# One-hot products in the order of the equalities, and the routing table's end half a step sooner, in a mixture-of-experts kernel on one core

## The chip, the cores and the metric

The kernel runs on one core of a Trainium2 chip. The metric is the time of one execution in microseconds (us) on the device. The engines of the core are named as in the profile: PE (TensorE, matmuls), PEld (its weight loads), DVE (VectorE), ACT (ScalarE), POOL (GpSimd) and SP (SyncE, which issues DMAs). L564 is line 564 of the kernel.

## The reference

`x` has 64 x 64 tokens of 256 numbers; each goes to 2 of 8 experts, and the result is added to `x`:

```python
xn = rms_w * (x * rsqrt(mean(x * x) + 1e-6))
gate_w = softmax(xn @ wg_W + wg_b + (cond @ gg_W + gg_b))     # 8 experts
topk_w, topk_i = top_k(gate_w, 2)
cw = sum(one_hot(topk_i) * topk_w)                            # weight of each expert
h1 = relu(x @ W1[e] + b1[e])                                  # 256 -> 512
h2 = relu(h1 @ W2[e] + b2[e])                                 # 512 -> 512
out = x + sum_e(cw[e] * (h2 @ W3[e] + b3[e]))                 # 512 -> 256
```

All inputs and the output are float32.

## The kernel before

**Tiles and units.** The kernel computes an expert only for the tokens that chose it. Tokens are sorted by expert into tiles of 128, and tiles into units of one expert. Units 0 to 7 (`E = 8`) are single tiles, one for each expert, made of the tokens of a first part (a quarter of all), which is routed first. The rest is routed while units 0 to 6 are computed, and gives units 8 and up, of 1 to 4 tiles each. A unit's rows are fetched from HBM by POOL's indirect DMAs (`gather`, `gather_unit`, L771), turned (for unit 8 by eight PE transposes, L836; for later units by a round through HBM, `stow` and `shuffle`, and DVE), taken through `layer1` (L939), `layer2` (L949) and `layer3` (L1076), scaled by DVE into `y` (L1090) and added to the output by POOL's indirect DMAs (`give`, L1091). Units of more than one tile use a fast product of blocks (`Fast`, L1030), whose `p(k)` are matmuls, `mix` and `fold` sums on DVE, and `c11` to `r21` the evaluations on DVE and ACT.

**The order.** All is written out by hand in one program order (`tc.manual_schedule()`); each engine, and each DMA queue, works through its own instructions in that order and waits by semaphore for the others. `head_step(u)` is the step of unit u from 0 to 6, `step(7)` follows, `step_fast` does units 8 and up. In a step PE computes layer 1 of unit u, transposes for unit u + 1, layer 3 of unit u - 1 and layer 2 of unit u.

**The routing of the rest** is a generator, `rest()`. `more(ns)` runs it until its yields, which name the estimated time of what they issued, add up to `ns`; at a `yield None` it stops for that call. A step calls `more(3200)` once or twice. Its last stretch makes the table of tokens: for each of 4 chunks (`NCH`) of 16 pairs (`GC`) a partition, DVE writes

- `ohl`, an equality of the rank in its tile with 0 to 127 (L688, 128 x 16 elements of f16 a partition),
- `ohh`, an equality of the tile's number with `whole` (L690, 69 x 16 elements, `NREST` = 69),
- `ohv`, `ohh` times the token's number (L695, 69 x 16 elements).

`ohl` and `ohh` have the pair as their innermost index, `ohv` the tile. For each of the 16 pairs one matmul (L564) has `ohl[:, :, g]` as the stationary operand (its columns lie 32 bytes apart) and `ohv[:, g, :]` as the moving one, and adds into 69 columns of a PSUM bank. `table(n)` issues the matmuls of the first n pairs that are at hand. Three sets of `ohl` and `ohv` are in turn; `ohh` is one buffer. After the last matmul four DVE instructions (L706 to L709) decode the table into `idxR`, the row numbers by which `gather_unit(E)` and `gather_unit(E + 1)` fetch units 8 and 9. After a `yield None` the generator goes on to the pairs' weights: `pB.exps` (ACT), `pB.weights` (DVE), `pB.spread` (POOL, which writes them to HBM for later gathers).

In `head_step` `table` is called ahead of layer 1 and ahead of layer 2: in step 5 with one and two chunks, in step 6 with three and four. The generator is run to the gathers (`while not fetched`) after layer 2 of step 6; in time, they follow the second `more(3200)` of that step. In the last `step` of a run of units, `layer3` and `give` of the last unit's tiles are called one by one, the upper half first.

Of the kernel before, what the change touches and what calls it, by code (L numbers as in the profile page):

```python
# [10 lines left out]
F16 = mybir.dt.float16  # L11
I32 = mybir.dt.int32
AF = mybir.ActivationFunctionType
ALU = mybir.AluOpType
# [7 lines left out]
def kernel(  # L22
# [18 lines left out]
    V = nc.vector  # L41
    P = 128
    B, S, H = x.shape
    G = cond.shape[1]
    E, _, M = W1.shape
# [5 lines left out]
    MC = M // P  # L51
# [5 lines left out]
    BT = 128  # L57
# [3 lines left out]
    NREST = (NPAIR - TOPK * BT + E * (BT - 1)) // BT  # L61
# [8 lines left out]
    GC = 16  # L70
    NCH = TOPK * NI // GC
# [37 lines left out]
    bigf = big.rearrange("p j k h -> p (j k h)")  # L109
    hid = [wall.tile([P, MC, SLOTS * BT], F32, name=f"hid{k}") for k in range(2)]  # L110
# [39 lines left out]
    tok16 = const.tile([P, NI], F16, name="tok16")  # L150
# [25 lines left out]
    def te(name, dt=F32):  # L176
        return buf(gx, [P, E], name, dt)
# [219 lines left out]
    fills, loads, fetches, fetched = [], [], [], []  # L397

    def load_weights(e, parts=(0, 1, 2)):
        for k in parts:  # L400
            dst, src = (
                (w1r[e % RING], W1[e].rearrange("(p c) m -> p c m", c=HC)),
                (w2a[:, e], W2[e].rearrange("(c p) n -> p c n", p=P)),
                (w3r[e % RING], W3[e].rearrange("(c p) h -> p c h", p=P)),
            )[k]
            loads.append(nc.sync.dma_start(dst, src))  # L406
# [137 lines left out]
    def third_part():  # L544

        turn(GA + 5, 1, 7, "V", 3)
        some(len(left))
        raw = upright()
        nc.scalar.copy(graw[:, NA : NA + 4 * TPB, :].rearrange("p (q k) e -> p q k e", q=4), raw)
        gates_2(((4, 5), (6, 7)), PB[7])  # L550
        nc.scalar.copy(gTs, PB[7])
# [6 lines left out]
    mms = []  # L558

    def table(n=TOPK * NI):  # L560

        while mms and mms[0][2] < n:
            lo, hi, g = mms.pop(0)
            nc.tensor.matmul(PB[7][:, 0:NREST], lhsT=lo, rhs=hi, start=(g == 0), stop=(g == TOPK * NI - 1))  # L564

    def rest():
# [15 lines left out]
        more, mm, base, offs, nbf = (te(a) for a in ("more", "mm", "base", "offs", "nbf"))  # L582
# [96 lines left out]
        LW, HW = P * GC // 2, NREST * GC // 2  # L679
        for c in range(NCH):  # L680
            cols = slice(c * GC, (c + 1) * GC)
            b0 = HW + (c % 3) * (LW + HW)
            ohh = bigf[:, 0:HW].bitcast(F16).rearrange("p (t g) -> p t g", g=GC)
            ohl = bigf[:, b0 : b0 + LW].bitcast(F16).rearrange("p (r g) -> p r g", g=GC)
            ohv = bigf[:, b0 + LW : b0 + LW + HW].bitcast(F16).rearrange("p (g t) -> p g t", g=GC)
            if c >= 3:
                table((c - 2) * GC)
            V.tensor_tensor(ohl, iotx, lo16[:, cols].unsqueeze(1).to_broadcast([P, P, GC]), ALU.is_equal)  # L688
            yield 1250
            V.tensor_tensor(  # L690
                ohh, whole, hi16[:, cols].unsqueeze(1).to_broadcast([P, NREST, GC]), ALU.is_equal
            )
            yield 750
            i0 = c * GC % NI
            V.tensor_tensor(  # L695
                ohv,
                ohh.rearrange("p t g -> p g t"),
                tok16[:, i0 : i0 + GC].unsqueeze(2).to_broadcast([P, GC, NREST]),
                ALU.mult,
            )  # L700
            for g in range(GC):
                mms.append((ohl[:, :, g], ohv[:, g, :], c * GC + g))
            yield 1300
        yield None
        table()
        V.tensor_scalar(sa, tab, 0.0, -1.0, ALU.is_gt, ALU.mult)  # L706
# [40 lines left out]
    def size(u):  # L747
        return 1 if u < E else sizes[u - E]
# [36 lines left out]
    def gather(b):  # L785
        fetches.append(fetch(ring(run, [P, H], "xg", 3, b), xrows, b))
# [8 lines left out]
    def gather_cw(u):  # L795
        for b in tiles(u):
            cg = cgs[b] = cgR[:, b % NCG]
            fetch(cg, (cwdA if b < E else cwdR)[:, :], b)
# [79 lines left out]
    def stream_1(u, engine=mybir.EngineType.Activation):  # L878
        e = expert(u, engine)
        QUEUES[engine].dma_start(w1r[u % RING], W1[e].rearrange("e (p c) m -> p (e c) m", c=HC))  # L880

    def stream_3(u, engine=mybir.EngineType.Activation):
        e = expert(u, engine)
        QUEUES[engine].dma_start(w3r[u % RING], W3[e].rearrange("e (c p) h -> p (e c) h", p=P))
# [7 lines left out]
    def stage_1(u):  # L892

        if u < E:
            ww[u] = [w1r[u % RING], vT[:, :, u, :], w2a[:, u], w3r[u % RING]]
            return
        e = ex[u] = expert(u, mybir.EngineType.DVE)
        bb = ring(run, [P, 2, MC], "bb", 3, u)
        V.tensor_copy(bb.unsqueeze(2), vT[:, :, e])
        ww[u] = [w1r[u % RING], bb, st2, w3r[u % RING]]  # L900
# [31 lines left out]
    def layer1(u):  # L932
        w1, bb = ww[u][0:2]
        w = len(tiles(u)) * BT
        cols = xT[:, :, slots(u), :].rearrange("p c s t -> p c (s t)")
        for m in range(MC):
            ph = PB[m][:, 0:w]
            for c in range(HC):
                nc.tensor.matmul(  # L939
                    ph, lhsT=w1[:, c, ts(m, P)], rhs=cols[:, c, :], start=(c == 0), stop=(c == HC - 1)  # L940
                )
            nc.scalar.activation(hid[0][:, m, 0:w], ph, AF.Relu, bias=bb[:, 0, m : m + 1])
# [124 lines left out]
    def sums(u, k):  # L1067

        bank, part = {1: (u % 2, 0), 4: (k // 2, k % 2)}.get(size(u), (k % 2, k // 2))
        return PB[5 + bank][:, ts(part, H)]  # L1070

    def layer3(u, which=None):
        w3 = ww[u][3]
        for k in which or range(size(u)):
            for n in range(MC):
                nc.tensor.matmul(  # L1076
                    sums(u, k), lhsT=hid[1][:, n, ts(k, BT)], rhs=w3[:, n, :], start=(n == 0), stop=(n == MC - 1)
                )

    def give(u, which=None):  # L1080
# [45 lines left out]
    def head_step(u, more):  # L1126

        if u + 3 < E:
            gather(u + 3)
        for k in range(3 * u, min(3 * u + 3, E)):  # L1130
            gather_cw(k)
        table(GC * max(0, 2 * u - 9))
        layer1(u)
        if u + RING < E:
            load_weights(u + RING, (0, 1))
        if u == 0:
            third_part()
        else:
            transpose_x(u + 1)
            stage_1(u + 1)  # L1140
            if u != 2:
                more(3200)
            scaled(u - 1, "A")
            layer3(u - 1)
            if u - 1 + RING < E:
                load_weights(u - 1 + RING, (2,))
            if u == 1:
                nc.sync.dma_start(b3_sb[:, 4:E], b3[4:E].unsqueeze(0).to_broadcast([P, E - 4, H]))
        table(GC * max(0, 2 * u - 8))
        if u == 0:  # L1150
            layer2(u, {1: last_upright, 2: lambda: transpose_x(1)})
            stage_1(1)
            more(3200)
        elif u == 2:
            layer2(u, {1: lambda: more(3200)})
        else:
            more(3200)
            layer2(u)
        if u == E - 2:
            while not fetched:  # L1160
                more(1000000)
            stream_3(E, mybir.EngineType.SP)
            fill(2)
            stream_1(E + 1, mybir.EngineType.SP)
            stow(E + 1)
            shuffle(E + 1)
            fill(3)
            give(u - 2)
        if u >= 1 and u != E - 3:
            give(u - 1)  # L1170
        if u == E - 3:
            stream_1(E, mybir.EngineType.SP)
        if u in (E - 4, E - 3):
            fill(u - (E - 4))
# [15 lines left out]
    def step(u, last):  # L1190

        far = fetches_of(u, last)
        if u < last:
            layer1(u)
            if u >= E:
                streams(u, last)
            stage_2(u)
        if u + 1 < last:
            gather_cw(u + 1)
        if u - 1 >= E:  # L1200
            scales(u - 1)
        scaled(u - 1)
        if u + 1 < last:
            stage_1(u + 1)
            if u + 1 > E:
                transpose_x(u + 1)
        if far:
            shuffle(u + 2)
        if u == last:
            for k in reversed(range(size(u - 1))):  # L1210
                layer3(u - 1, [k])
                give(u - 1, [k])
            return
        layer3(u - 1)
        if u == E - 1:
            stream_1(E + 2, mybir.EngineType.SP)
            stream_3(E + 1, mybir.EngineType.SP)
        if u + 1 == E:
            transpose_x(u + 1)
        give(u - 1)  # L1220
# [116 lines left out]
    with tc.manual_schedule():  # L1337
# [17 lines left out]
        for u in range(E - 1):  # L1355
            head_step(u, routing)
# [56 lines left out]
```

## Time and profile before

| | |
|---|---|
| median of 3 runs | 480.58 us (480.06 to 482.44) |
| the profiled execution | 481.13 us, of which the profile's span has 479.3 |
| PE busy | 461.5 us, 96% of the span |
| DVE, ACT, POOL busy | 71%, 46%, 55% |
| mean granted TensorE clock | 0.991 |
| chain that ended last, by engine | PE 79%, DMA 9%, issue 6%, POOL 2% |
| L695, the product `ohv` | 4 times 2162 ns |
| L690, the equality `ohh` | 4 times 731 ns |
| L688, the equality `ohl` | 4 times 1220 ns |
| L564, the table's matmuls | 64, 4.6 us busy |

Times in the profile count from the span's start. A group's line gives the engine, the operation, the tiles written and read (out<-in), the shapes and the count, then busy time and mean length. In a timeline a bracket at the end of a line is the time that the engine stood idle ahead of the instruction, and what released it. Unit 8's layer 1 begins at 94.68 us, and PE's last matmul of all at about 469 us.

### The profile page before, as it was taken

The page shows a single profiled execution, that of the slowest core. Times are in us where ns is not written, and L with a number is a line of the kernel's source. Part 1 is how long each engine was busy: PE and PEld are TensorE (multiplying, and loading weights), DVE is VectorE, ACT ScalarE, POOL GpSimd, SP SyncE. Part 2 cuts the span into 40 slices and gives each one's busy share as a digit, 9 for nine tenths or more (in the row PEclk, how much of TensorE's full clock was granted, in tenths as well). Part 3 has the DMA queues.
Part 4 walks back from the last instruction along what each step waited for, and adds up shares of the span by engine and source line. Part 5 has one row for each costly group of instructions (what it writes and reads, how often), then busy time and mean ns, then how long its engine had stood idle before and what let it go on. Part 6 is the DMA issues. An engine that isn't in the chain of part 4 may idle for free.

```text
span 479.3 us, 8619 instructions
## 1 busy us (share of the span) xinstructions
PE 461.5 (96%) x2750; PEld 418.6 (87%) x2750; DVE 338.5 (71%) x883; ACT 219.9 (46%) x510; POOL 261.5 (55%) x229
## 2 busy tenths in 40 slices
PE   7899999799999999999999999999999999999991
PEld 5689989668888888888888889999999999999991
DVE  6896994446758585766767566786776778988850
ACT  5744534134444343526262626255264455565550
POOL 3356243647787877373638182855645535664222
PEclk9999999899999999999999999999999999999997
DMA  8699999662766665554646354655744554565221
GB/s 318 227 338 375 367 375 382 174 222 56 222 130 178 123 166 124 137 125 133 116 133 109 108 114 108 116 145 121 171 120 101 129 143 83 166 167 130 61 25 22
DMA packets 75900, 78.59 MB, mean 164 GB/s; under 512 B 35231, under 2 KB 64386, under 8 KB 75460
## 3 DMA queue, kind: packets, MB, share of 16 engines
q1 hardware_dynamic: 48976, 43.29, 27.3%
q0 software_dynamic: 15232, 17.34, 21.5%
q10 hardware_dynamic: 11636, 17.32, 11.2%
q8 instruction: 23, 0.38, 0.3%
q14 instruction: 33, 0.27, 0.2%
HBM read 62.46 MB, written 20.45 MB: 173 GB/s over the span
## 4 chain that ended last, share of the span: by engine, by line
PE 79%; DMA 9%; issue 6%; POOL 2%; DVE 1%; SPq 1%; ACT 0%; POOLq 0%; DVEq 0%
PE pb L1030 54%; PE pb L1076 21%; DMA out_dram<-in_x_dram 3%; DMA out_dram<-y,idxA 3%; PE pb L939 1%; DMA xgE<-in_x_dram,idxR 1%; POOL out_dram L1091 1%; PE pb L949 1%; DMA big<-in_x_dram 1%; DMA out_dram<-y,idxR 1%; SPq L406 1%; PE pb L207 1%; DMA xg<-in_x_dram,idxA 1%; POOL cg L771 0%; PE pb L238 0%
## 5 line engine op out<-in xcount | busy, mean ns | idle before, releaser
L1091 POOL DMA_INDIRECT out_dram<-y,idxR x59 | 95.6, 1620 | 113.7 <-DVE y L1090 55.4
L1076 PE MATMUL pb<-w3r,hid 128*128 128x256 f32 x536 | 125.5, 380 | 0.2 <-ACT hid L1051 0.2
L1076 PEld LDWEIGHTS pb<-w3r,hid 128*128 128x128 f32 x536 | 99.3, 190 | 13.5 <-issue 0.5
L1051 ACT ACTIVATE hid<-hid,bb 128x256 f32<-128x256 f32 (+4 forms) x148 | 71.8, 534 | 32.3 <-DVE hid L1048 28.5
L1030 PE MATMUL pb<-hid,big 128*128 128x256 f32 (+2 forms) x456 | 86.3, 332 | 0.0
L1030 PEld LDWEIGHTS pb<-hid,big 128*128 128x128 f32 x456 | 74.1, 191 | 5.2
L771 POOL DMA_INDIRECT cg<-cwdR,idxR x59 | 61.7, 1046 | 25.6 <-issue 18.7
L1039 ACT COPY q1s<-pb 128x512 f32<-128x512 f32 (+2 forms) x54 | 26.2, 485 | 76.0 <-PE pb L1030 75.6
L1039 ACT COPY big<-pb 128x512 f32<-128x512 f32 (+2 forms) x57 | 27.9, 490 | 68.1 <-PE pb L1030 68.1
L1030 PE MATMUL pb<-mixB,big 128*128 128x256 f32 (+2 forms) x304 | 57.6, 332 | 0.0
L1030 PE MATMUL pb<-hotA,big 128*128 128x256 f32 (+2 forms) x304 | 54.5, 332 | 0.0
L1030 PEld LDWEIGHTS pb<-mixB,big 128*128 128x128 f32 x304 | 49.2, 191 | 3.3
L1030 PEld LDWEIGHTS pb<-hotA,big 128*128 128x128 f32 x304 | 48.7, 191 | 3.3
L1030 PE MATMUL pb<-mixX,iotx 128*128 128x256 f32 (+2 forms) x216 | 44.7, 330 | 0.0
L771 POOL DMA_INDIRECT xgE<-in_x_dram,idxR x31 | 32.6, 1051 | 20.7 <-DVE idxR L709 9.7
L1030 PEld LDWEIGHTS pb<-mixX,iotx 128*128 128x128 f32 x216 | 36.3, 191 | 2.8
L771 POOL DMA_INDIRECT big<-in_x_dram,idxR x28 | 30.2, 1080 | 8.5 <-issue 7.9
L1090 DVE SCALAR_TENSOR_TENSOR y<-pb,cw,bc 128x256 f32<-128x256 f32 x59 | 27.5, 478 | 9.9 <-PE pb L1076 8.8
L1051 ACT ACTIVATE hid<-pb,bb 128x256 f32<-128x256 f32 (+2 forms) x74 | 27.2, 419 | 14.6 <-PE pb L1030 14.6
L949 PEld LDWEIGHTS pb<-hid,w2a 128*128 128x128 f32 x256 | 30.9, 198 | 1.0 <-issue 0.8
L949 PE MATMUL pb<-hid,w2a 128*128 128x128 f32 x256 | 31.8, 282 | 0.0
L1030 PE MATMUL pb<-xT,w1r 128*128 128x256 f32 (+2 forms) x144 | 29.8, 330 | 0.0
(286 smaller groups left out, 647.9 us busy)
## 6 DMA issues: line engine op xcount, KB each, us to landing
w3r<-in_L_cond_W_dram ACTq DMA_DIRECT2D x17, 512.0 KB, 4.8
w2a<-in_L_cond_W_dram SPq DMA_DIRECT2D x8, 1024.0 KB, 12.9
w1r<-in_L_cond_W_dram ACTq DMA_DIRECT2D x16, 512.0 KB, 3.3
w1r<-in_L_cond_W_dram SPq DMA_DIRECT2D x11, 512.0 KB, 12.0
w3r<-in_L_cond_W_dram SPq DMA_DIRECT2D x10, 512.0 KB, 11.1
gTs<-scr SPq DMA_DIRECT2D x7, 512.0 KB, 4.2
out_dram<-in_x_dram SPq DMA_DIRECT2D x4, 768.0 KB, 10.8
big<-in_x_dram SPq DMA_DIRECT2D x4, 512.0 KB, 4.6
```

The source lines that it names most:

```text
L207: nc.tensor.transpose(TB[bank][:, ts(k, P)], xin[j][:, k, ts(c, P)], ident)
L406: loads.append(nc.sync.dma_start(dst, src))
L771: return nc.gpsimd.indirect_dma_start(out=dst, out_offset=None, in_=src, in_offset=bass.IndirectOffsetOnAxis(ap=index(b), axis=0), bounds_ ...
L939: nc.tensor.matmul(ph, lhsT=w1[:, c, ts(m, P)], rhs=cols[:, c, :], start=(c == 0), stop=(c == HC - 1))
L949: nc.tensor.matmul(ph, lhsT=w2[:, m, ts(n, P)], rhs=hid[0][:, m, 0:BT], start=(m == 0), stop=(m == MC - 1))
L1030: nc.tensor.matmul(bank[:, ts(n, self.w)], lhsT=w[:, c, ts(n, P)], rhs=x[:, c], start=new and n == 0 and c == 0, stop=n == HB - 1 and c == ...
L1039: nc.scalar.copy(self.q[(1, 6, 5).index(k)], self.tall(self.X if k == 5 else self.U))
L1051: nc.scalar.activation(out, src, AF.Relu, bias=ww[self.u][1][:, self.l, n : n + 1])
L1076: nc.tensor.matmul(sums(u, k), lhsT=hid[1][:, n, ts(k, BT)], rhs=w3[:, n, :], start=(n == 0), stop=(n == MC - 1))
L1090: V.scalar_tensor_tensor(y, sums(u, k), cw, bc, ALU.mult, ALU.add)
L1091: add = nc.gpsimd.indirect_dma_start(out=orows, out_offset=bass.IndirectOffsetOnAxis(ap=index(b), axis=0), in_=y, in_offset=None, bounds_c ...
```

## The change

The product `ohv` gets the order of `ohh`, with the pair innermost; DVE then reads and writes it packed, and a matmul's moving operand `ohv[:, :, g]` has its 69 columns 32 bytes apart. The yield behind it says 750 instead of 1300. `table` is called with one chunk ahead of layer 1 of step 5, with three ahead of layer 2 of step 5, and with all four ahead of layer 1 of step 6, where the generator is also run up to the gathers. `layer3` takes an order of its sum's four parts; for tiles of the upper half of the last unit the order is 2, 3, 0, 1.

```diff
-            ohv = bigf[:, b0 + LW : b0 + LW + HW].bitcast(F16).rearrange("p (g t) -> p g t", g=GC)
+            ohv = bigf[:, b0 + LW : b0 + LW + HW].bitcast(F16).rearrange("p (t g) -> p t g", g=GC)
...
-            V.tensor_tensor(
-                ohv,
-                ohh.rearrange("p t g -> p g t"),
-                tok16[:, i0 : i0 + GC].unsqueeze(2).to_broadcast([P, GC, NREST]),
-                ALU.mult,
-            )
+            V.tensor_tensor(ohv, ohh, tok16[:, i0 : i0 + GC].unsqueeze(1).to_broadcast([P, NREST, GC]), ALU.mult)
             for g in range(GC):
-                mms.append((ohl[:, :, g], ohv[:, g, :], c * GC + g))
-            yield 1300
+                mms.append((ohl[:, :, g], ohv[:, :, g], c * GC + g))
+            yield 750
...
-    def layer3(u, which=None):
+    def layer3(u, which=None, order=range(MC)):
         w3 = ww[u][3]
         for k in which or range(size(u)):
-            for n in range(MC):
+            for i, n in enumerate(order):
                 nc.tensor.matmul(
-                    sums(u, k), lhsT=hid[1][:, n, ts(k, BT)], rhs=w3[:, n, :], start=(n == 0), stop=(n == MC - 1)
+                    sums(u, k), lhsT=hid[1][:, n, ts(k, BT)], rhs=w3[:, n, :], start=(i == 0), stop=(i == MC - 1)
                 )
...
-        table(GC * max(0, 2 * u - 9))
+        table(GC * {E - 3: 1, E - 2: NCH}.get(u, 0))
+        if u == E - 2:
+            while not fetched:
+                more(1000000)
         layer1(u)
...
-        table(GC * max(0, 2 * u - 8))
+        table(GC * (NCH - 1) * (u == E - 3))
...
         if u == E - 2:
-            while not fetched:
-                more(1000000)
             stream_3(E, mybir.EngineType.SP)
...
             for k in reversed(range(size(u - 1))):
-                layer3(u - 1, [k])
+                layer3(u - 1, [k], (2, 3, 0, 1) if 2 * k >= size(u - 1) else range(MC))
                 give(u - 1, [k])
```

## The prediction

> **What bounds the kernel now.** I read the page first: PE is busy for 96% of the span, the chain that ended last is 79% PE, so what counts is PE's idle time and slow time. The list of PE's waits from 55 us on has only three lines (columns: who waits, for what, us in total, times, longest):
>
> ```profile
> PE pb L836 <- DMA xgE<-in_x_dram,idxR: 2.5, 4, 0.9
> PE pb L564 <- DVE big L695: 0.8, 1, 0.8
> PE pb L1076 <- ACT hid L1051: 0.2, 1, 0.2
> ```
>
> All three lie on places that the change touches, and after 95 us PE has no other wait: what is gained in the head should reach the end. Next, PE's timeline around them (start, length):
>
> ```profile
> 62.77 1.18 PE L564 MATMUL pb<-big 128*128 128x69 f16 x16 [0.78 <-DVE big L695]
> ...
> 77.02 1.13 PE L564 MATMUL pb<-big 128*128 128x69 f16 x16
> 77.99 3.82 PE L949 MATMUL pb<-hid,w2a 128*128 128x128 f32 x32
> 81.64 1.95 PE L939 MATMUL pb<-xT,w1r 128*128 128x128 f32 x16
> 83.43 1.89 PE L1076 MATMUL pb<-w3r,hid 128*128 128x256 f32 x8
> 86.02 0.39 PE L836 MATMUL pb<-ident,xgE 128*128 128x128 f32 x1 [0.70 <-DMA xgE<-in_x_dram,idxR]
> ...
> 88.99 1.34 PE L836 MATMUL pb<-ident,xgE 128*128 128x128 f32 x5 [0.94 <-DMA xgE<-in_x_dram,idxR]
> 90.12 4.72 PE L949 MATMUL pb<-hid,w2a 128*128 128x128 f32 x32
> 94.68 7.03 PE L939 MATMUL pb<-xT,w1r 128*128 128x512 f32 x16
> ```
>
> The eight transposes of unit 8 should follow layer 3 at about 85.2, but stand until 88.99 for the rows of its fourth tile; and the same layer 2 that took 3.65 us from start to next start at 77.99 takes 4.56 at 90.12. The windows say why (columns: length, PE, PEld, DVE, ACT, POOL busy, granted clock, DMA share, GB/s): the clock falls after the stall.
>
> ```profile
> 87.50:90.00 2.50, 1.40 (x6) 1.21 (x7) 0.49 (x1) 0.00 (x0) 1.89 (x3) 0.75 0.40 120
> 90.00:92.50 2.50, 2.50 (x15) 2.50 (x14) 2.46 (x5) 0.95 (x2) 1.52 (x1) 0.56 0.34 65
> ```
>
> Why are the rows late? DVE's and POOL's timelines show the chain: the last product of a one-hot ends at 75.0, the table's last matmuls stand on PE behind layer 3 (77.02), the decoding follows at 78.19, the gathers start at 79.36, and the fourth, issued at 83.32, lands at 88.94 by the chain of waits.
>
> ```profile
> 58.66 1.22 DVE L688 TENSOR_TENSOR big<-iotx,lo 128x2048 f16<-128x2048 f16 x1
> 59.80 0.73 DVE L690 TENSOR_TENSOR big<-whole,hi 128x1104 f16<-128x1104 f16 x1
> 60.56 2.15 DVE L695 TENSOR_TENSOR big<-big,tok 128x1104 f16<-128x1104 f16 x1
> 62.62 1.22 DVE L688 TENSOR_TENSOR big<-iotx,lo 128x2048 f16<-128x2048 f16 x1
> ...
> 78.19 0.23 DVE L706 TENSOR_SCALAR sa<-pb 128x69 f32<-128x69 f32 x1 [3.17 <-PE pb L564]
> ```
> ```profile
> 79.36 1.04 POOL L771 DMA_INDIRECT xgE<-in_x_dram,idxR  x1 [9.68 <-DVE idxR L709]
> ...
> 83.32 1.00 POOL L771 DMA_INDIRECT xgE<-in_x_dram,idxR  x1 [0.30 <-issue]
> ```
>
> **The products on DVE.** Four products take 2162 ns each; in the new order they have the form of the equality with `whole` (f16, 1104 elements, both inputs packed in the inner dimension), which takes 731 ns. From start to next start an equality with `iotx` is 1.14 us, one with `whole` 0.76; so a chunk takes 1.14 + 0.76 + 0.76 = 2.66 us instead of 3.96. With the smaller yields the routine hands out more per call: chunk 1's second equality goes ahead of `y` of unit 3 (0.40 us), chunk 2's product and all of chunk 3 come half a step earlier. Products are ready at 60.56 + 0.73 = 61.3 (chunk 0), 64.4, 67.0 and 69.7 us (was 62.7 to 75.0).
>
> **PE until the transposes.** PE came free at 62.77 - 0.78 = 61.99; chunk 0 is now there, so 0.78 us is saved. From 61.99: chunk 0 1.01, layer 1 1.87, transposes 0.23, layer 3 1.73 (starts of the timeline), at 66.8 chunks 1 and 2 together (2 x 0.97; chunk 2 wanted at 67.8, ready at 67.0), layer 2 3.65, and at 72.42 chunk 3 before layer 1 of unit 6: done at 73.4. The same 64 products stand on PE, so the transposes are reached at 85.16 - 0.78 = 84.38.
>
> **The gathers.** Decoding started 0.20 us after the next matmul's start (77.99 to 78.19) and the first gather 1.17 us after it, so now 73.39 + 0.20 + 1.17 = 74.76, against 79.36: 4.60 us sooner, with POOL idle then. The fourth ends its issue at 74.76 + 3.96 + 1.00 = 79.7. Before, the first gather landed 5.6 us after its issue ended, with the DMA share over 1.0, and the fourth 4.6 us after, with the share at 0.64. The new ones lie wholly in the full stretch, so I take 5.6: landed at 85.3. PE wants that tile after three transposes (0.115 each, from the pair at 75.06), at 84.73. Left is 0.59 us of wait. With 4.6 it would be nothing; with the 6.75 us that the scatter-add issued at 67.47 took, 1.74. The stall with its transposes was 85.16 to 90.12, 4.96 us; eight transposes need 0.92, so 4.04 - 0.59 = 3.45 is saved. A wait of 0.59 is under the 0.78 at 62 us, after which the clock stayed 1.00; so layer 2 of unit 7 goes back to 3.65: another 0.91.
>
> **TensorE at a stride.** The moving operand's 69 columns now lie 32 bytes apart. No row shows a moving operand so. The pace is (1.18 - 0.23) / 15 = 63 ns for each product, while the stationary operand is already read at 32 bytes. Lower bound: no change, since 69 columns even at the rate of f32 ones (layer 3: 1.73 us / 8 / 256 = 0.84 ns a column) take 58 ns and hide in 63; they were packed before, so no gain. Upper bound: DVE's own read at this step, 2162 / 1104 = 1.96 ns an element, so 135 ns: +72 x 64 = 4.6 us. I take the lower, for the stationary operand's reads are the nearest row, and keep 4.6 for the range. [...]
>
> **What else moves.** The exponents (ACT 0.35 + 0.21 us) and weights (DVE, 1.9 us from 82.56 to 84.44) now stand in step 6: both engines idle there (ACT 2.81 us before layer 2, DVE 3.17); without cover they'd cost at most their own 2.4 us. On DVE, behind the decoding's wait for PE, stand these weights and `y` of units 4 and 5, wanted only before layer 3 of unit 6 rewrites the bank at 82.6. On POOL the spreading of weights (95.63 to 99.3) now stands ahead of the scatter-adds of units 4 and 5, behind the eight gathers (84.9): those adds start at about 89.2, as before (89.83), and the weight gathers, which waited 6.00 us for the spread until 105.29, come sooner. SP's order is the same: its store of unit 9's rows can't be later than 91.34, and their shuffled copy landed at 100.5, wanted by DVE at 107.28 - 5.1 = 102.2.
>
> **The end.** In the last unit the first tile's sums begin with the upper half, whose outputs were ready at 465.05, instead of waiting for ACT: 0.23 us, and POOL's last scatter follows PE through `y`.
>
> **The sum**: 0.78 + 3.45 + 0.91 + 0.23 = 5.4 us. The profiled execution took 481.13 us (span 479.3): 475.75. It was 0.55 over the median of three, 480.58; the forecast against the median is 475.2.
>
> **Rivals.** (1) *Gathers land late all the same.* The rows stay as slow as that scatter-add: wait 1.74, and the clock falls once more: 5.96 - 1.74 - 0.91 = 3.3 us, 477.3. For: DMA share 1.0 to 85 us. Against: the gathers' own rows, 4.6 to 5.6. (2) *The strided read shows*, at DVE's rate: 5.4 - 4.6 = 0.8 us, 479.8: no change that can be told. For: DVE's row. Against: the stationary operand, read at the same step within 63 ns. (3) *Slower by the strided read.* If the whole pace stretches by DVE's ratio 2162 / 731 = 2.96, 63 becomes 186 ns, 64 x 123 = 7.9 us on PE: 2.5 us slower, 483.1. It decides from 63 + 5.4 / 64 = 147 ns a product. (4) *The products aren't faster* (DVE stays at 2.16 us): then chunk 2 is ready at 71.06 (68.89 + 2.17), but PE wants it, now ahead of layer 2 of unit 5, at 67.8 + 0.78 = 68.6, and waits 2.5 us; the gathers start at 78.0, the transposes at 87.7, their fourth tile lands at 88.6, layer 2 of unit 7 starts at 89.2 instead of 90.12: 0.9 + 0.91 + 0.23 = 2.0 us, 478.6. Against: the row of the same form.
>
> **How the numbers follow.** Forecast 0.78; rival 1 0.09; rivals 2 and 4 0.08 together; rival 3 0.05. The forecast's own range is 474.1 (no wait left, 5.96 us, from the median less the 0.52 by which the lowest run lies below it) to 476.4 (wait 1.74, clock kept). Rival 1 with half a microsecond of scatter sets the upper end, 477.8; outside lie rivals 2 to 4. Faster by over 0.5% (2.4 us, about what a measurement of this kernel can tell from no change): 0.78 + 0.09 = 0.87; within: 0.08; slower: 0.05.
>
> **What would show it.** Right: the products at 0.73 us; the table's last chunk on PE near 72.4; the first xgE gather near 74.8; under 0.8 us of wait before the transposes, at about 84.4; layer 2 of unit 7 in 3.65 us at clock 1.00; no wait at the last layer 3. Wrong: a pace of the products well over 63 ns; gathers landing over 6 us after issue; a new PE wait after 90 us, on unit 9's rows above all.

## The result and the profile after

The changed kernel takes 482.47 us (median of 22 runs, 480.37 to 484.85) where the kernel before takes 480.54 (22 runs): a ratio of 1.0037, 95% interval 1.0025 to 1.005. The forecast was 475.2. The profiled execution took 481.46 us, its span 479.7.

PE's waits from 55 us on are down to one line: the wait for the first product and the one in the last layer 3 are gone, and 0.7 us is left of 2.5 ahead of unit 8's transposes (layer 3 is now at L1071, the transposes at L831).

```profile
PE pb L831 <- DMA xgE<-in_x_dram,idxR: 0.7, 1, 0.7
```

So PE lost nearly all its idle time, as forecast, and the kernel still became slower, by 1.9 us in the medians of this pair. PE's timeline (start, length) shows where the time went:

```profile
62.01 2.25 PE L564 MATMUL pb<-big 128*128 128x69 f16 x16
64.08 1.97 PE L934 MATMUL pb<-xT,w1r 128*128 128x128 f32 x16
...
67.85 4.39 PE L564 MATMUL pb<-big 128*128 128x69 f16 x32
72.06 5.37 PE L944 MATMUL pb<-hid,w2a 128*128 128x128 f32 x32
77.26 2.27 PE L564 MATMUL pb<-big 128*128 128x69 f16 x16
79.35 1.97 PE L934 MATMUL pb<-xT,w1r 128*128 128x128 f32 x16
...
90.21 0.51 PE L831 MATMUL pb<-ident,xgE 128*128 128x128 f32 x3
91.39 0.87 PE L831 MATMUL pb<-ident,xgE 128*128 128x128 f32 x5 [0.67 <-DMA xgE<-in_x_dram,idxR]
92.09 3.74 PE L944 MATMUL pb<-hid,w2a 128*128 128x128 f32 x32
95.67 7.03 PE L934 MATMUL pb<-xT,w1r 128*128 128x512 f32 x16
```

Sixteen products took 1.18 us and now take 2.25. From start to next start the four chunks hold PE for 2.07 + 4.21 + 2.09 = 8.37 us instead of 1.01 + 3 x 0.97 = 3.92. That is 4.45 us more. It is counted as busy time, which is why no wait shows it. And layer 2 of unit 5, behind the 32 products, took 5.20 us instead of 3.65. The windows (length, PE, PEld, DVE, ACT, POOL, granted clock, DMA share, GB/s) show the clock at half there, while PE was never idle:

```profile
67.50:70.00 2.50, 2.50 (x20) 2.40 (x19) 1.70 (x3) 0.00 (x0) 1.07 (x1) 1.00 1.04 394
70.00:72.50 2.50, 2.50 (x19) 2.50 (x18) 0.00 (x0) 0.00 (x0) 0.70 (x1) 0.91 1.07 383
72.50:75.00 2.50, 2.50 (x13) 2.50 (x13) 0.00 (x0) 0.37 (x1) 0.00 (x0) 0.50 1.07 358
```

On DVE the products are as short as forecast (first line), but the decoding (second line) comes after DVE stood idle for 10.33 us, at the end for PE. POOL's first gather therefore starts later than before, not sooner (the third and fourth line are POOL's):

```profile
60.60 0.73 DVE L695 TENSOR_TENSOR big<-big,tok 128x1104 f16<-128x1104 f16 x1
...
79.57 0.23 DVE L701 TENSOR_SCALAR sa<-pb 128x69 f32<-128x69 f32 x1 [10.33 <-PE pb L564]
```
```profile
80.74 1.04 POOL L766 DMA_INDIRECT xgE<-in_x_dram,idxR  x1 [10.04 <-DVE idxR L704]
...
84.70 1.00 POOL L766 DMA_INDIRECT xgE<-in_x_dram,idxR  x1 [0.30 <-issue]
```

At the end PE passes from the last block product to layer 3 without a wait: 0.89 us from start to start, where it was 465.81 - 464.52 = 1.29 (before, the first two lines; after, the last two).

```profile
464.52 1.06 PE L1030 MATMUL pb<-mixB,big 128*128 128x128 f32 x8
465.81 3.72 PE L1076 MATMUL pb<-w3r,hid 128*128 128x256 f32 x16 [0.23 <-ACT hid L1051]
```
```profile
465.51 1.06 PE L1025 MATMUL pb<-mixB,big 128*128 128x128 f32 x8
466.40 3.62 PE L1071 MATMUL pb<-w3r,hid 128*128 128x256 f32 x16
```

### The profile page after: what moved, and what is told of

The parts are those of the page before. It is cut to its first block, busy times and chain, and to the rows that moved or that the text cites. A ratio compares the mean times of both kernels' runs of the same rounds, so it can differ in the third digit from the quotient of the medians.

```text
span 479.7 us, 8621 instructions
## 1 busy us (share of the span) xinstructions
PE 464.8 (97%) x2750; PEld 423.2 (88%) x2750; DVE 332.4 (69%) x883; ACT 220.4 (46%) x510; POOL 261.6 (55%) x229
## 4 chain that ended last, share of the span: by engine, by line
PE 79%; DMA 10%; issue 6%; POOL 2%; DVE 1%; SPq 1%; ACT 0%; ACTq 0%; POOLq 0%; DVEq 0%
PE pb L1025 54%; PE pb L1071 21%; DMA out_dram<-in_x_dram 3%; DMA out_dram<-y,idxA 3%; PE pb L934 1%; DMA xgE<-in_x_dram,idxR 1%; POOL out_dram L1086 1%; DMA out_dram<-y,idxR 1%; SPq L406 1%; PE pb L944 1%; DMA gTs<-in_L_cond_rms_w_dram 1%; PE pb L207 1%; DMA xg<-in_x_dram,idxA 1%; POOL cg L766 0%; PE pb L238 0%
## 5 line engine op out<-in xcount | busy, mean ns | idle before, releaser
L1071 PE MATMUL pb<-w3r,hid 128*128 128x256 f32 x536 | 125.4, 379 | 0.0
L1071 PEld LDWEIGHTS pb<-w3r,hid 128*128 128x128 f32 x536 | 99.4, 190 | 13.1 <-issue 0.5
```

Source lines behind the costliest of these rows:

```text
L1071: nc.tensor.matmul(sums(u, k), lhsT=hid[1][:, n, ts(k, BT)], rhs=w3[:, n, :], start=(i == 0), stop=(i == MC - 1))
```

## The experiments

Theory S: the change lost to the strided moving operand, over which PE takes twice as long. Rival P: it lost to the new place of table, decoding and gathers. Each kernel was timed against the kernel before on the same chip, and the ratios below are of that kind; they are not simply the quotients of the two medians. On two of the chips the kernel before itself took 490.75 and 501.54 us. All six traces there of kernels with the change's placement show PE taking 6.7 to 7.4 us from layer 1 of unit 7 to the layer 3 behind it, where it takes 1.8 in the quieter chips' traces and in e1_order_only, the one trace there with the old placement. Most of that goes to waits such as this one of e2_place_only (a line of PE's waits from 85 to 96 us). What causes them isn't known, and the kernel before has no trace on these chips, so it isn't shown whether the new place brings them there. From these chips I take the paces of the products (the time from one product's start to the next one's), and the times with care.

```profile
PE pb L939 <- issue: 2.1, 1, 2.1
```

**One part alone: the order, and the place.** The first is the kernel before with the three lines of the product's order (the yield stays 1300); the second is the changed kernel with those three lines taken back:

```diff
-            ohv = (...).rearrange("p (g t) -> p g t", g=GC)
+            ohv = (...).rearrange("p (t g) -> p t g", g=GC)
-            V.tensor_tensor(ohv, ohh.rearrange("p t g -> p g t"), <tok16 along t>, ALU.mult)
+            V.tensor_tensor(ohv, ohh, <tok16 along t>, ALU.mult)
-                mms.append((ohl[:, :, g], ohv[:, g, :], c * GC + g))
+                mms.append((ohl[:, :, g], ohv[:, :, g], c * GC + g))
```

> Only the order of the products is changed (packed on DVE, 69 moving columns 32 bytes apart on PE); calls of the table, yields and the last layer 3 are as before. Theory S (the strided moving operand costs PE 66 ns a product): L695 takes 0.73 us, the pace of L564 is 129 ns, PE stands 64 x 66 = 4.2 us longer under the products, the wait of 0.78 us ahead of chunk 0 is gone; the gathers start about 3.4 us later than before, so PE reaches unit 8's transposes later by as much and waits as long as before: about 3 to 4 us slower than before. Rival P (the placement of the table calls is what lost the gain): this kernel is faster than before by the 0.78 us or equal to it.

> Everything of the change but the order of the products: DVE writes them as before (2.16 us), PE reads 69 packed columns. Theory S: pace 63 ns, clock 1.00 from 70 to 77 us, a wait of about 2.5 us for chunk 2 ahead of layer 2 of unit 5, the gathers start near 78.0 us instead of 79.36, 0.6 us or less of wait ahead of unit 8's transposes: about 2 us faster than before. Rival P: as slow as the changed kernel or slower, about 2 us over before.

Measured on the 490.75 us chip, with six runs each: the order alone 1.0169 (1.0087 to 1.0252), which is 8.3 us where 3 to 4 were expected; the place alone 1.0132 (1.0068 to 1.0197), 6.5 us slower where 2 us faster was expected. The pace settles half of it: with the order alone 16 products take 2.25 us as in the changed kernel, (2.25 - 0.313) / 15 = 129 ns each; with the place alone 1.13 us, so 60 ns. The longer product goes with the order. The place alone came out slower here, against theory S, but with the waits named above in its trace; it was repeated below.

**The stride by itself: 16, 8 and 4 bytes.** The changed kernel, but equality, product and `whole` lie in groups of `GL` pairs, so that DVE still reads and writes packed and the 69 columns lie 2 x GL bytes apart:

```diff
+    GL = 4
-    whole = const.tile([P, NREST, GC], F16, name="whole")
+    whole = const.tile([P, GC // GL, NREST, GL], F16, name="whole")
...
-            ohh = (...).rearrange("p (t g) -> p t g", g=GC)
+            ohh = (...).rearrange("p (h t l) -> p h t l", h=GC // GL, l=GL)
-            ohv = (...).rearrange("p (t g) -> p t g", g=GC)
+            ohv = (...).rearrange("p (h t l) -> p h t l", h=GC // GL, l=GL)
...
-                mms.append((ohl[:, :, g], ohv[:, :, g], c * GC + g))
+                mms.append((ohl[:, :, g], ohv[:, g // GL, :, g % GL], c * GC + g))
```

(`hi16` and `tok16` are given to DVE in the same groups, and ACT's copy fills `whole` so.) That columns in the same 16 bytes (a line, in the expectations) are paid for once is the author's assumption, on trial here; what the runs show of it are the paces below, 69 ns with two columns to 16 bytes and 129 with one.

> The changed kernel, but the products (and the equalities with whole) lie in groups of 4 pairs, so that the moving columns are 8 bytes apart instead of 32, and DVE still reads and writes packed. Theory S with 16-byte lines (a column that shares its line with another is free): pace 63 ns, products on DVE 0.73 us, no clock fall, and the forecast's gain: 5 us faster than before. Rival S' (any step other than 1 costs the same): pace 129 ns and the time of the changed kernel, 2 us over before.

> As the kernel with 8 bytes, but groups of 8 pairs: columns 16 bytes apart, each in a line of its own. Theory S with 16-byte lines: pace 129 ns as at 32 bytes, clock fall behind the 32 products, time as the changed kernel. If the cost follows the bytes stepped over instead (a wider line, or a rate of so many bytes): a pace between 63 and 129 ns.

> The changed kernel with groups of 2 pairs: the moving columns 4 bytes apart, four to a line of 16 bytes. If only the reads of new lines cost: two to a line gave 67 ns, so 63 to 67 ns here and the time of the kernel with 8 bytes, 475.5 to 477. If DVE loses its packed rate in runs of 4 bytes, its equality and product with 1104 elements take over 1.2 us, and part of the gain goes.

The 32 products of two chunks in PE's timeline, at 16 bytes (e4_step16):

```profile
69.94 4.32 PE L565 MATMUL pb<-big 128*128 128x69 f16 x32
```

at 8 bytes (e3_step8):

```profile
70.82 2.40 PE L565 MATMUL pb<-big 128*128 128x69 f16 x32
```

and at 4 bytes (g2_step4):

```profile
70.57 2.14 PE L565 MATMUL pb<-big 128*128 128x69 f16 x32
```

The pace is the length less that of one matmul, by the number of steps:

| columns apart | columns in 16 bytes | pace of 128x69 f16 |
|---|---|---|
| 2 bytes (before) | 8 | (1.13 - 0.229) / 15 = 60 ns |
| 4 bytes | 4 | (2.14 - 0.230) / 31 = 62 ns |
| 8 bytes | 2 | (2.40 - 0.252) / 31 = 69 ns |
| 16 bytes | 1 | (4.32 - 0.310) / 31 = 129 ns |
| 32 bytes (the change) | 1 | (4.39 - 0.313) / 31 = 132 ns |

The step from 8 to 16 bytes nearly doubles the time of a product, and from 16 to 32 almost nothing more comes. Counted by the pieces of 16 bytes that hold a column, 129 ns for 69 pieces is 1.9 ns each, and 69 ns for 35 is 2.0, an estimate from these two paces. It fits a price for each piece, and not one for the bytes stepped over; how the columns are read no trace shows. With fewer pieces the products keep 60 to 62 ns; what sets that is not shown either. No step between 8 and 16 bytes was tried. The times on the same chips: 16 bytes 1.0086 (1.0042 to 1.0131), 8 bytes 0.9975 (0.9921 to 1.0029), 4 bytes on the other chip 0.9928 (0.9852 to 1.0004). So 8 bytes missed the 5 us that were expected: its trace has the waits in unit 7 too, and its time can't be told from no change here. DVE kept 0.73 us a product at 4 bytes.

**All four corners on one quiet chip.** The changed kernel, the changed kernel with 8 bytes, the place alone, and the order alone with 8 bytes.

> The changed kernel itself once more, beside the three that take it apart. Theory S (columns in lines of their own cost PE 66 ns a product; the time lost there, 64 x 66 = 4.2 us, eats the gain): pace 129 ns, 1 to 2 us slower than before. The half clock behind the 32 products together: if it needs a whole window of 3.41 us within the 4.2 us that they take, it falls in some executions only, and where it doesn't, layer 2 of unit 5 takes 3.6 us and the kernel is about equal to before.

> The changed kernel with the moving columns 8 bytes apart (four to a group, two to a line of 16 bytes). Theory S: pace 67 ns, products at 0.73 us on DVE, no fall of the clock; PE reaches unit 8's transposes near 84.6 us, waits up to 1 us for the gathers: 4 to 5 us faster than before, 5 to 7 us faster than the changed kernel. Rival P (the new place of the table, the decoding and the gathers costs what it brings, whatever the products cost): within 1 us of before.

> All of the change but the order of the products. Theory S: the wait for chunk 2 on PE is about 2.2 us ahead of layer 2 of unit 5, the gathers start about 1.3 us sooner than before: 1 to 2 us faster than before. Rival P: slower than before by 1 us or more.

> Only the order of the products, with columns 8 bytes apart; the table calls, the yields and the last layer 3 as before. Theory S: the wait ahead of chunk 0 goes, 0.78 us, the gathers start and are wanted 0.6 us sooner each, so the stall ahead of unit 8's transposes stays: 0.5 to 1 us faster than before. Rival P: as much faster as the whole change with 8 bytes, or more.

The kernel before took 481.13 us here (median). The fourth column is read from PE's timelines: the start of unit 8's layer 1 less that of unit 4's layer 2, which leaves out the scatter of what comes ahead (unit 4's layer 2 starts at 58 to 61 us).

| | median | ratio, 95% interval | layer 2 of unit 4 to layer 1 of unit 8 |
|---|---|---|---|
| before | 481.13 us | | 94.68 - 58.25 = 36.43 us |
| changed (f1) | 482.02 us | 1.0007, 0.9989 to 1.0026 | 97.49 - 59.26 = 38.23 us |
| changed, 8 bytes (f2) | 476.24 us | 0.9897, 0.9871 to 0.9922 | 91.58 - 60.23 = 31.35 us |
| place alone (f3) | 480.66 us | 0.9992, 0.9976 to 1.0008 | 94.17 - 59.47 = 34.70 us |
| order alone, 8 bytes (f4) | 480.49 us | 0.9983, 0.9968 to 0.9998 | 94.34 - 60.70 = 33.64 us |

(The stretch of before is that of the trace shown with the prediction. Each stretch is that of one execution.) With the stride mended and the placement and the end kept, the change brings 4.9 us by the medians, and the stretch is 36.43 - 31.35 = 5.08 us shorter. On a quiet chip rival P is out, and this version beats both kernels. From f1 to f2 the stretch loses 6.88 us: the products take 4.40 us instead of 8.37, layer 2 behind the 32 takes 3.64 instead of 5.21, and the wait ahead of the transposes is 0.25 instead of 1.67. The changed kernel itself is not told from before here, nor on the chip of h2_after below: the 1.9 us of the first pair did not come again. PE's timeline of f2_step8:

```profile
63.80 1.26 PE L565 MATMUL pb<-big 128*128 128x69 f16 x16
...
68.70 2.40 PE L565 MATMUL pb<-big 128*128 128x69 f16 x32
70.92 3.80 PE L950 MATMUL pb<-hid,w2a 128*128 128x128 f32 x32
74.56 1.27 PE L565 MATMUL pb<-big 128*128 128x69 f16 x16
...
86.55 0.51 PE L837 MATMUL pb<-ident,xgE 128*128 128x128 f32 x3
87.31 0.86 PE L837 MATMUL pb<-ident,xgE 128*128 128x128 f32 x5 [0.25 <-DMA xgE<-in_x_dram,idxR]
88.01 3.74 PE L950 MATMUL pb<-hid,w2a 128*128 128x128 f32 x32
```

Layer 2 behind the 32 products takes 3.64 us from start to start, the transposes wait 0.25 us, and layer 2 behind them takes 3.57.

Neither half brings much alone by the medians: 0.6 us for the order (expected 0.5 to 1), 0.5 for the place (expected 1 to 2), which its interval doesn't tell from nothing. The stretches are shorter by 2.79 and 1.73 us, so they do not follow the medians here. One reason can be that the single trace of before has the clock at 0.50 from 88.77 to 92.18 us, which other executions may lack; it isn't settled. The trace of the place alone shows what holds it back: with the slow product on DVE PE waits for chunk 0 and, in the new place, for chunk 2:

```profile
64.13 1.19 PE L564 MATMUL pb<-big 128*128 128x69 f16 x16 [0.93 <-DVE big L695]
...
72.32 1.13 PE L564 MATMUL pb<-big 128*128 128x69 f16 x16 [2.21 <-DVE big L695]
```

and with the order alone the gathers still start behind layer 3, and PE waits for all four tiles, 1.7 us in all (the first of the four lines of f4_order8_only):

```profile
87.86 0.39 PE L837 MATMUL pb<-ident,xgE 128*128 128x128 f32 x1 [0.63 <-DMA xgE<-in_x_dram,idxR]
```

**The half clock.** One line more in the changed kernel separates the 32 products; it was run on two chips, the second time beside the changed kernel. The 8-byte kernel was repeated with the first.

```diff
+            table(GC * 2 * (u == E - 3))
             scaled(u - 1, "A")
             layer3(u - 1)
```

> The changed kernel (columns 32 bytes apart) with one more call of the table: chunk 1 stands ahead of layer 3 of unit 4 and chunk 2 behind it, so no more than 16 products (2.1 us) stand together. [...] The pace stays at 129 ns.

> The kernel with 8 bytes once more, beside the other two: 4 to 5 us faster than before, pace 67 ns, no fall of the clock before 95 us.

> The changed kernel (columns 32 bytes apart) with chunk 1 ahead of layer 3 of unit 4 and chunk 2 behind it: no more than 16 products (2.1 us) stand together. If 32 products together let the clock fall, it stays at 1.00 here until the transposes of unit 8, layer 2 of unit 5 takes 3.6 us, and the kernel is 0.5 to 1.6 us faster than the changed one beside it (the more often it falls there, the more). If the fall has another cause, the two are equal.

> The changed kernel beside it. In its two traces so far the clock fell to half behind the 32 products, and layer 2 of unit 5 took 5.2 us instead of 3.65. If a whole window has to lie within the 4.2 us of the products, there are executions without the fall, and the times lie apart by about 1.6 us.

On the 501.54 us chip: separated 0.9981 (0.987 to 1.0093), which decides nothing; 8 bytes again 0.9903 (0.9837 to 0.9969), as on the quiet chip. On a quiet chip (before: 481.81 us): separated 0.9997 (0.9977 to 1.0017), changed 1.0004 (0.9991 to 1.0017). In the traces of this second pair the clock was 1.00 in every window from 65 to 80 us. PE's timeline of h2_after, behind its 32 products:

```profile
68.84 4.39 PE L564 MATMUL pb<-big 128*128 128x69 f16 x32
73.05 3.75 PE L944 MATMUL pb<-hid,w2a 128*128 128x128 f32 x32
76.64 2.29 PE L564 MATMUL pb<-big 128*128 128x69 f16 x16
```

Layer 2 takes 3.59 us here, against 5.20 in the profiled execution of the changed kernel and 5.21 in f1_after_again, so the fall comes in some executions and not in others. By that length it shows behind the products in these two of the three traces of the changed kernel, and in none of the kernels with 16 bytes, with chunks apart or with a short pace, where the same layer 2 takes 3.59 to 3.66 us. The mean clock recorded with each run fits. It is 0.991 in the two traces with the fall and 0.995 in h2_after. Of the changed kernel's twelve runs beside f2_step8 one has 0.995, and it is the fastest, 480.28 us; of the twelve on h2_after's chip five have 0.994 or 0.995, with a median of 480.78, and the seven others 481.89. The six of f2_step8 have 0.992 to 0.995. In the clock records of the profiled executions of the changed kernel and of the kernel before, the times from one change of the clock to the next are 64.85, 3.41 and 399.36 us, and 81.92, 3.41 and 382.29: 19, 1, 117, 24, 1 and 112 times 3.413 us, the window of the expectations. In the changed kernel's, the 3.41 us ahead of the fall (68.63 to 72.04 us) lie within the 32 products (67.85 to 72.06). That the products are the cause is not shown: separating them moved the median by 0.5 us, which is less than the pair can tell.

## Why the prediction was wrong

**The bound, right.** The three waits named were the time to be had, and it reaches the end: f2_step8 has two of them gone and 0.25 us left of the third, and is 4.9 us faster; the forecast was 5.4.

**The products on DVE, right**: 0.73 us each, the last ready at 69.2 (forecast 69.7).

**The order on PE, right**: chunk 0 without a wait at 62.01 (forecast 61.99), chunks 1 and 2 without a wait.

**TensorE at a stride: the step that failed.** Two ends were worked out, 0 and 4.6 us, and the lower one taken. Measured are 8.37 - 3.92 = 4.45 us. So the term was near its upper end: DVE's 1.96 ns for an element at 32 bytes and PE's 1.9 ns for a column are the same within 5%. The reason for the other end was that the stationary operand is read at the same step within 63 ns (60 in three of the four chunks). That row says nothing of a moving column's price: 128 columns one behind the other at 1.9 ns would take 243 ns, more than the whole pace, so they are read in another way; in which, no run here shows. Of the moving columns the runs show that a product with two of them to each 16 bytes costs 69 ns, with one 129.

**The clock, not priced.** The sum gave back 0.91 us for a clock that stays up, and had no term for one that falls elsewhere. In the profiled execution it fell behind the 32 products, and layer 2 of unit 5 took 1.55 us more; why it fell stays open. The fall lasted 3.41 us at 0.50 (72.04 to 75.45 us), and PE had no idle time in it or in the 4.21 us of products ahead of it.

Together: 5.4 - 4.45 - 1.55 is 0.6 us slower than 481.13, 481.7; the profiled execution took 481.46. The median of 22 runs lies 1.0 us above that one, which no trace explains, and on two other chips the changed kernel was not told from before.

**The gathers, right but late by as much as PE.** They began at 80.74 instead of 74.76, for the table ended 6 us later; the fourth landed 91.35 - 85.70 = 5.65 us after its issue (taken: 5.6) and PE waited 0.67 (0.59). Layer 2 of unit 7 took 3.58 us at clock 1.00 (3.65). With PE late by 5.8 us and the gathers by 6.0, the wait is short but both are late.

**What else moves, right**: no PE wait behind the 0.7 us, not for unit 9's rows either. **The end**: 0.40 us from start to start (0.23).

**The rivals.** Rival 2, the strided read at DVE's rate, is what happened, with the clock on top; it was given less than 0.08. Its forecast, 479.8, lacked the clock. Rival 3's larger price (186 ns) didn't come: that the median lies near its 483.1 says nothing for it.

## What to carry to other kernels

When a change packs an operand for one engine, ask at which step the other engine will read it, and time that step. At 32 bytes DVE paid 1.96 ns an element and PE 1.9 a column here (DVE was timed at this step and packed only), and with groups of four 16-bit elements both were quick: 0.73 us a product on DVE, 69 ns on PE. Where an unseen price is bounded by two rows and the sum hangs on it, ask which row has the same pattern of reads: here it was another engine's, and the row of the same engine, for its other operand, misled. One case is no rule, so keep the dearer end in the range. The slower matmuls showed here as 4.45 us more of busy time and not as a wait, so a list of waits that gets shorter is no proof of a gain.

## What the runs showed of the hardware that was not expected

- Moving columns of f16 at steps of 2, 4, 8, 16 and 32 bytes: 60, 62, 69, 129 and 132 ns for a 128x69 matmul behind a weight load.
- In the profiled execution of the changed kernel the clock fell to 0.50 for 3.41 us behind 4.21 us in which PE, by the profile, was busy all the time with strided products. Layer 2 behind them took 5.20 us there and 5.21 in f1_after_again, but 3.59 in h2_after.
